# STU's products by disjoint segments of a block, with four stored sums of the mixed matrices

## The chip, the cores and the metric

The kernel runs on one core of a Trainium2 chip. The metric is the device time of one execution in microseconds, the median of several; everything is fp32. The engines named here are TensorE (matrix products, PE in the profile), VectorE (DVE), ScalarE (ACT), GpSimd (POOL) and SyncE (SP), which issues most of the transfers.

## The reference, cut to what matters

The input is a batch of 4 images of 48 x 48 tokens with 128 channels. A first layer (group norm, projection, depthwise convolution, four directional selective scans, gating) and an attention over the 2304 tokens come first. The change lies in the last part, an STU (a spectral filter bank) that runs on four prefixes of the sequence and adds the four results with weights:

```python
for i, frac in enumerate((1, 2, 4, 8)):
    xi = x[:, :T // frac]
    si = _stu(xi, sigma, phi, M_u[i], M_phi_plus[i], M_phi_minus[i])
    si = jnp.pad(si, ((0, 0), (0, T - si.shape[1]), (0, 0)))
    outs.append(si)
...
return jnp.sum(stacked * weights, axis=-1)
```

`_stu` convolves the tokens causally with 16 filters `phi`, in a plain and in an alternating form, multiplies each result by the 128 x 128 matrices `Mpp[k]` and `Mpm[k]` with weight `sigma**0.25`, and adds three products of delayed tokens with `Mu`. The convolution is causal, so its values don't depend on where a prefix ends; only the matrices differ. For a token at position t the result is therefore one product with the weighted sum of the matrices of those prefixes that hold t: all four in the first eighth (288 tokens), three up to a quarter (576), two up to a half (1152), one beyond.

## The kernel before, in words

Per batch the kernel runs a prologue, the scans, an epilogue with the attention, and the STU. The scans of batch b run beside other work for TensorE: beside those of batch 0 the matrices are mixed (`mixture`), beside those of batches 1, 2 and 3 runs the STU of the batch before. The STU of batch 3 runs alone at the end (`stu_alone`, the last stage).

The order on each engine is written out by hand. `scans` makes 192 steps per batch (24 chunks of 384 tokens with 8 units each). Each step has one scan unit: a product with `B` (VectorE at L450, or GpSimd for three units of eight), four decays on ScalarE (`dA`, L455), four scans on VectorE (L458), a product with `C` on GpSimd (L467) and a sum on TensorE (L475). At four points of a step the function `more` draws pieces of the accompanying work until that work has had its share of all TensorE columns. The total is 24 `CHUNK_COLS` (147456 columns) plus `MIX_COLS` or `STU_COLS`, so each step gets the same number of columns, whatever it takes in time.

The STU takes every fourth token as one column (576 columns in four residues). The columns are cut into five blocks, `BLOCKS`: 128, 128, 128, 128 and 64 wide. An item is one block with one filter `k`; there are 5 x 16 items per batch. An item has six convolution groups (`conv`, L978), each a chain of 128 x 256 matmuls (128 x 128 in the last block), one for every block up to this one. Their operand `tt` is fetched in a ring of four buffers (`fetch`, L948), and the matrices `G` of the item in a ring of two (`fetch_G`, L959), right behind the `tt` of three items later. After three groups of an item stands `project` of the item before (L1044): for each of two halves `q` the eight convolved pieces `U` are multiplied by `G`, and all 16 filters add into one bank of PSUM. `ar` (L1034) puts the products with `Mu` (tile `mue`) into the same bank at the start of a block. Copies of convolution results are made by ScalarE (L992, L1004), sums of them by VectorE (L1007).

Three of the places where a prefix ends fall inside a block: after 72 columns of block 0, 16 of block 1 and 32 of block 2 (`extra` in `BLOCKS`). The kernel before takes the product of the whole block with the sum of the matrices of all prefixes that hold the whole block, and adds for the first `extra` columns a product with the one matrix that holds only there. `parts(w, extra)` gives these two, (128, 1) and (extra, 0), the numbers 1 and 0 being matrices of the pair that was fetched. To serve them, DRAM keeps six matrices for each filter and half (`gd`) and for each delay (`mud`): three partial sums and three single ones.

`mixture` makes `gd`. For each filter and half it scales a unit matrix by the weights, on ScalarE (`W`, L821 and L822), and multiplies it with the matrices `M` (L835): twelve matmuls in two groups (j = 1 the sums, six matmuls of 384, 256 and 128 columns; j = 0 the single ones, six of 128 columns), two copies to `Gm` by ScalarE (L810) and one store (L812). The load of `M` (L817) is issued just ahead of the first matmul that uses it.

Of the kernel before, what the change touches and what calls it, by code (L numbers as in the profile page):

```python
# [8 lines left out]
F32 = mybir.dt.float32  # L9
AF = mybir.ActivationFunctionType  # L10
ALU = mybir.AluOpType
# [4 lines left out]
P = 128  # L16
B, H, W, C = 4, 48, 48, 128
# [8 lines left out]
KF = 16  # L26
NF = 4
# [6 lines left out]
SLOT = 2 * (LF + 1)  # L34


BLOCKS = [(0, 128, 0, 72), (128, 256, 2, 16), (256, 384, 4, 32), (384, 512, 5, 0), (512, 576, 5, 0)]
SHIFT = 55.0


# [14 lines left out]
def hybrid_kernel(ctx: ExitStack, tc: tile.TileContext, a: dict, out: bass.AP):  # L55
# [3 lines left out]
    nc = tc.nc  # L59
# [3 lines left out]
    res = ctx.enter_context(tc.tile_pool(name="res", bufs=1, space=DRAM))  # L63
# [70 lines left out]
    zs = res.tile([NH, P, L], F32, name="zd")  # L134
    td = res.tile([L, C], F32, name="td")
    ud = res.tile([P, 4, 1 + LF], F32, name="ud")
    gd = res.tile([KF, P, 2, 2 * NF - 2, C], F32, name="gd")
    mud = res.tile([P, 2 * NF - 2, 3, C], F32, name="mud")
    fd = res.tile([KF, 3, 2, LF + P], F32, name="fd")
    xdd = [[res.tile([P, CS], F32, name=f"xdd{k}_{c}") for c in range(L // CS)] for k in range(2)]  # L140

# [587 lines left out]

    MIX_COLS = KF * 2 * 2 * (6 + 3) * C

    ws = wp.tile([P, KF, NF], F32, name="ws")

    def weights(one):

        def load(name, shape, src):  # L740
            t = one.tile(shape, F32, name=name)
            nc.scalar.dma_start(t, src)
            return t

        lg = load("lg", [P, NF], a["log_weights"].partition_broadcast(P))
        gu = load("gu", [P, NF], a["gumbel"].partition_broadcast(P))
        sg = load("sg", [P, KF], a["sigma"].partition_broadcast(P))
        ph = load("ph", [KF, 2, 2, LF + P + 1], a["phi"])
        mu = load("mu", [P, NF, 3, C], a["M_u"].rearrange("i j d e -> d i j e"))
        for i in range(6):  # L750
            yield
        hard, wts = [one.tile([P, NF], F32, name=n) for n in ("hard", "wts")]
        m = one.tile([P, 2], F32, name="m")

        nc.vector.tensor_add(lg, lg, gu)
        nc.vector.tensor_reduce(m[:, 0:1], lg, AX.X, ALU.max)
        nc.vector.tensor_scalar(lg, lg, m[:, 0:1], None, ALU.subtract)
        nc.scalar.activation(lg, lg, AF.Exp)
        yield

        fc = one.tile([KF, 3, 2, LF + P], F32, name="fc")
        n = LF + P
        nc.vector.tensor_copy(fc[:, 0], ph[:, :, 0, :n])
        yield
        nc.vector.tensor_sub(fc[:, 1], ph[:, :, 1, 1:], ph[:, :, 0, :n])
        yield
        nc.vector.tensor_sub(fc[:, 2], ph[:, :, 1, :n], ph[:, :, 0, :n])
        nc.scalar.dma_start(fd, fc)
        yield
        nc.vector.tensor_reduce(m[:, 0:1], lg, AX.X, ALU.add)  # L770
        nc.vector.reciprocal(m[:, 0:1], m[:, 0:1])
        nc.vector.tensor_scalar_mul(lg, lg, m[:, 0:1])
        nc.vector.tensor_reduce(m[:, 0:1], lg, AX.X, ALU.max)
        nc.vector.tensor_scalar(hard, lg, m[:, 0:1], None, ALU.is_equal)
        nc.vector.memset(m[:, 1:2], 1.0)
        yield
        for i in range(NF):

            nc.vector.tensor_tensor(hard[:, i:i + 1], hard[:, i:i + 1], m[:, 1:2], ALU.mult)
            nc.vector.tensor_tensor(m[:, 1:2], m[:, 1:2], hard[:, i:i + 1], ALU.subtract)  # L780
        nc.vector.tensor_sub(wts, hard, lg)
        nc.vector.tensor_add(wts, wts, lg)
        yield

        quarter = one.tile([P, KF], F32, name="quarter")
        nc.vector.memset(quarter, 0.25)
        nc.gpsimd.tensor_tensor(sg, sg, quarter, ALU.pow)
        mum = one.tile([P, 2 * NF - 2, 3, C], F32, name="mum")
        nc.vector.tensor_scalar_mul(mum[:, 5], mu[:, 0], wts[:, 0:1])
        for i in range(1, NF):  # L790
            nc.vector.tensor_scalar_mul(mum[:, 6 - 2 * i], mu[:, i], wts[:, i:i + 1])
            if i < NF - 1:
                nc.vector.tensor_tensor(mum[:, 5 - 2 * i], mum[:, 7 - 2 * i], mum[:, 6 - 2 * i], ALU.add)
            yield
        nc.scalar.dma_start(mud, mum)
        for i in range(NF):
            nc.vector.tensor_scalar_mul(ws[:, :, i], sg, wts[:, i:i + 1])
        zero = one.tile([P, 4, 1], F32, name="zero")
        nc.vector.memset(zero, 0.0)
        nc.scalar.dma_start(ud[:, :, 0:1], zero)  # L800

    def mixture(pool, ps):

        late = []
        banks = [0]

        def keep_(G, p, j, k, q):
            nc.scalar.copy(G[:, :, j], p)  # L810
            if j == 0:
                nc.sync.dma_start(gd[k, :, q], G.rearrange("p s j c -> p (s j) c"))  # L812

        for k in range(KF):
            M = [pool.two.tile([P, NF, C], F32, tag=f"M{j}", name=f"M{j}_{k}") for j in range(2)]
            for t, src in zip(M, ("M_phi_plus", "M_phi_minus")):
                nc.sync.dma_start(t, a[src][:, k].rearrange("i d e -> d i e"))  # L817

            W = pool.two.tile([P, 2, NF, P], F32, tag="W", name=f"W{k}")
            for i in range(NF):  # L820
                nc.scalar.activation(W[:, 0, i], ident, AF.Copy, scale=ws[:, k, i:i + 1])  # L821
                nc.scalar.activation(W[:, 1, i], nident, AF.Copy, scale=ws[:, k, i:i + 1])  # L822
            yield 0
            for q in range(2):
                G = pool.two.tile([P, 3, 2, C], F32, tag="Gm", name=f"Gm{k}_{q}")
                for j in (1, 0):
                    p = ps.psc.tile([P, 3, C], F32, tag=("c", "q0", "q1")[banks[0] % 3], name=f"G{k}_{q}_{j}")
                    banks[0] += 1
                    for i in range(NF):

                        n = NF - 1 - i if j else 1
                        if i == (NF - 1 if j else 0):
                            continue
                        for t in range(2):
                            nc.tensor.matmul(p[:, :n] if j else p[:, NF - 1 - i], W[:, q if t else 0, i],  # L835
                                             M[t][:, i].unsqueeze(1).to_broadcast([P, n, C]) if j else M[t][:, i],
                                             start=(t == 0 and (i == 0 or not j)),
                                             stop=(t == 1 and (i == NF - 2 or not j)))
                            yield n * C
                    if late:  # L840
                        keep_(*late.pop())
                    late.append((G, p, j, k, q))
        keep_(*late.pop())

    def begin_stu(b):
# [6 lines left out]
    def tail(b, J, T, po, pool, ps):  # L852
# [38 lines left out]
        for j in range(4):  # L891
# [5 lines left out]
        nc.sync.dma_start(ud[:, :, 1 + P * J:1 + P * J + k], uT.rearrange("c (j p) -> c j p", j=4))  # L897

    STU_COLS = sum(KF * 12 * sum(hi - max(lo, J * P) for J in range((hi + P - 1) // P))
                   + (2 * KF + 3) * 4 * (hi - lo + extra) + 4 * (hi - lo) for lo, hi, place, extra in BLOCKS)  # L900

    def stu(b, pool, ps):

# [15 lines left out]
        tts, Gs, Q, U, now, nxt = {}, {}, {}, {}, {}, [0]  # L919
        late = []  # L920
        banks = {}
# [98 lines left out]

        def parts(w, extra):

            return ((w, 1), (extra, 0)) if extra else ((w, 0),)

        def ar(n):

            (lo, hi, place, extra), k = items[n]
            w = hi - lo
            p = ps.psp.tile([P, 512], F32, tag="p", name=f"pr{b}_{n}")
            now["p"] = p = p[:, :4 * w].rearrange("p (f r m) -> p f r m", f=2, r=2)  # L1030
            for i, (v, x) in enumerate(parts(w, extra)):
                for j in range(3):
                    src = now["x"][:, 2 - j:6 - j].rearrange("p (r f) m -> p f r m", f=2)
                    nc.tensor.matmul(p[:, :, :, :v], now["mu"][:, x, j, :], src[:, :, :, :v],  # L1034
                                     start=(i == 0 and j == 0), stop=False)
            yield 3 * 4 * (w + extra)

        def project(n):
            (lo, hi, place, extra), k = items[n]
            w = hi - lo  # L1040
            p = now["p"].rearrange("p f r m -> p (f r) m")
            for q in range(2):
                for v, x in reversed(parts(w, extra)):
                    nc.tensor.matmul(p[:, :, :v], Gs[n][:, q, x, :], U[n][:, 4 * q:4 * q + 4, :v], start=False,  # L1044
                                     stop=(k == KF - 1 and q == 1 and v == w))
                yield 4 * (w + extra)
            if k == KF - 1:
                late.append(lambda: kept(n, now["p"], w))

# [83 lines left out]
    for b in range(B):  # L1133
        sp = Stage(tc, f"h{b}", "left", s=(6, SB))
        ps = Stage(tc, f"b{b}", "right", psa=(2, PSUM), psy=(1, PSUM), psB=(1, PSUM), psc=(1, PSUM), psp=(1, PSUM))
# [106 lines left out]
```

## Time and profile before

The time is 6407.89 us, median of 3 runs from 6407.33 to 6413.88; the profiled execution spans 6402.6 us.

| | busy us | share of the span |
|---|---|---|
| TensorE | 5427.8 | 85% |
| VectorE | 4622.7 | 72% |
| GpSimd | 3840.5 | 60% |
| ScalarE | 2980.6 | 47% |

| group | instructions | busy us | mean ns |
|---|---|---|---|
| projections L1044, all forms | 2048 | 693.5 | 468 |
| products with `mue` L1034, all forms | 192 | 65.8 | 493 |
| mixing matmuls L835, 128 columns | 512 | 106.6 | 340 |
| mixing matmuls L835, 256 columns | 128 | 52.3 | 496 |
| mixing matmuls L835, 384 columns | 128 | 79.0 | 722 |
| `Gm` copies L810 | 64 | 30.0 | 470 |

An fp32 matmul of the program stands in the trace as two records, each with a weight load, so 2048 records are 1024 matmuls. A record's duration runs to the end of the matmul, which overlaps with the next one's start; what a matmul takes of TensorE is read from the distance between starts, or from the chain of waits. The profile cuts the span into 40 slices of 160 us and gives the busy share of each engine in tenths. Idle time is put down to what ended it.

### The profile page before, as it was taken

What the parts mean: (1) busy time and instruction counts of PE and PEld (TensorE: products, weight loads), DVE (VectorE), ACT (ScalarE), POOL (GpSimd) and SP (SyncE); (2) the same over time, 40 slices, a digit from 0 to 9 for tenths busy, and PEclk for the clock granted to TensorE, in tenths of its full rate; (3) what the DMA queues carried; (4) which work ended last, traced back from release to release, by engine and by line L of the source; (5) the groups of instructions that cost most, each with busy time, mean ns of one, the idle gap of its engine ahead of it and who ended that gap; (6) DMA issues with size and microseconds to landing.
All of it is one profiled execution on the core that took longest, in us unless ns stands there. A gap on an engine that the chain in (4) does not pass through costs nothing.

```text
span 6402.6 us, 75570 instructions
## 1 busy us (share of the span) xinstructions
PE 5427.8 (85%) x25032; PEld 3364.4 (53%) x25032; DVE 4622.7 (72%) x5553; ACT 2980.6 (47%) x5693; POOL 3840.5 (60%) x1825
## 2 busy tenths in 40 slices
PE   3665565697999998888999998788999998889999
PEld 1222222444556667544555666534555667547889
DVE  6999999548889998458899998458899998311000
ACT  2555555245555554245555554245555554232111
POOL 1988888406788887307788987207888987100000
PEclk6778777799999999899999999899999999899999
DMA  4556566127888888127888888127888887025546
GB/s 106 139 138 151 141 143 149 40 55 167 196 203 214 225 218 244 53 62 172 197 205 218 226 220 236 41 64 188 195 214 215 219 230 218 28 70 150 153 141 212
DMA packets 658246, 1033.52 MB, mean 161 GB/s; under 512 B 93856, under 2 KB 515872, under 8 KB 633120
## 3 DMA queue, kind: packets, MB, share of 16 engines
q1 hardware_dynamic: 652032, 1025.00, 62.3%
q10 hardware_dynamic: 5824, 3.69, 0.2%
q8 instruction: 200, 3.28, 0.2%
q14 instruction: 190, 1.56, 0.1%
HBM read 905.79 MB, written 122.56 MB: 161 GB/s over the span
## 4 chain that ended last, share of the span: by engine, by line
PE 49%; DVE 20%; DMA 17%; POOL 4%; issue 4%; ACT 4%; SPq 3%; DVEq 0%; ACTq 0%; POOLq 0%
PE cv L978 22%; DVE s L458 8%; PE pr L1044 7%; DMA tt<-fd 6%; DMA rep<-dtdud 4%; PE y L475 4%; DVE s L450 4%; PE s L714 4%; DMA bc<-xdd 3%; PE o L707 3%; POOL s L467 3%; PE B L442 2%; PE op L650 2%; DVE xc L264 2%; DMA G<-gd 2%
## 5 line engine op out<-in xcount | busy, mean ns | idle before, releaser
L467 POOL TENSOR_TENSOR s<-s,bc 128x1536 f32<-128x1536 f32 x768 | 2646.4, 3447 | 177.3 <-DVE s L458 93.3
L458 DVE TENSOR_TENSOR_SCAN s<-dA,carry,s 128x384 f32<-128x384 f32 x2560 | 2442.5, 1000 | 246.3 <-ACT dA L455 244.1
L455 ACT ACTIVATE dA<-rep,A 128x384 f32<-128x384 f32 x3072 | 1780.5, 585 | 1422.4 <-DVE s L458 1395.7
L978 PE MATMUL cv<-tt,u 128*128 128x256 f32 (+3 forms) x7680 | 1649.9, 354 | 131.2 <-DMA tt<-fd 68.1
L978 PEld LDWEIGHTS cv<-tt,u 128*128 128x128 f32 x7680 | 1271.9, 193 | 647.2 <-issue 309.2
L450 POOL TENSOR_TENSOR s<-rep,bc 128x1536 f32<-128x1536 f32 x288 | 993.9, 3451 | 93.0 <-DMA bc<-xdd 93.0
L450 DVE TENSOR_TENSOR s<-rep,B 128x1536 f32<-128x1536 f32 x480 | 832.7, 1735 | 78.3 <-PE B L442 47.1
L978 PE MATMUL cv<-tt,us 128*128 128x256 f32 (+3 forms) x3840 | 855.4, 352 | 35.2 <-DMA tt<-fd 26.0
L475 PE MATMUL y<-s,csum 128*32 128x384 f32 x6144 | 714.7, 540 | 139.7 <-DVE ya L481 75.8
L978 PEld LDWEIGHTS cv<-tt,us 128*128 128x128 f32 x3840 | 640.6, 192 | 228.9 <-issue 66.7
L1007 DVE TENSOR_TENSOR U<-cv,Q 128x256 f32<-128x256 f32 (+1 forms) x640 | 244.4, 382 | 688.3 <-PE cv L978 679.9
L1044 PE MATMUL pr<-U,G 128*128 128x512 f32 (+4 forms) x2048 | 693.5, 468 | 2.2 <-ACT U L1004 2.2
L442 PE MATMUL B<-xd,spread 128*128 128x384 f32 x960 | 446.9, 550 | 182.9 <-DVE s L450 173.1
L1004 ACT COPY U<-cv 128x256 f32<-128x256 f32 (+1 forms) x640 | 222.9, 348 | 676.1 <-PE cv L978 675.2
L458 DVE TENSOR_TENSOR_SCAN s<-dA,s 128x384 f32<-128x384 f32 x512 | 458.4, 941 | 77.1 <-ACT dA L455 76.1
L466 POOL COPY carry<-s 128x4 f32<-128x4 f32 x640 | 120.9, 189 | 560.8 <-DVE s L458 536.4
L1044 PEld LDWEIGHTS pr<-U,G 128*128 128x128 f32 x2048 | 336.3, 190 | 194.3 <-issue 140.4
L992 ACT COPY Q<-cv 128x256 f32<-128x256 f32 (+3 forms) x640 | 223.0, 348 | 378.7 <-PE cv L978 375.2
L714 PE MATMUL s<-xnT 128*128 128x512 f32 (+1 forms) x720 | 356.9, 581 | 44.7 <-ACT xnT L676 23.4
L158 POOL TENSOR_TENSOR ln_vu<-ln_vu,mhalf 128x4 f32<-128x4 f32 (+1 forms) x20 | 26.8, 1340 | 603.4 <-DVE ln_vu L157 603.4
L475 PEld LDWEIGHTS y<-s,csum 128*32 128x32 f32 x6144 | 126.7, 112 | 492.9 <-issue 328.7
L716 ACT ACTIVATE e<-s,shift 128x512 f32<-128x512 f32 (+1 forms) x360 | 230.9, 644 | 315.2 <-PE s L714 314.7
(158 smaller groups left out, 3976.5 us busy)
## 6 DMA issues: line engine op xcount, KB each, us to landing
rep<-dtdud SPq DMA_DIRECT2D x768, 384.0 KB, 7.7
tt<-fd SPq DMA_DIRECT2D x192, 577.0 KB, 5.3
bc<-xdd SPq DMA_DIRECT2D x2304, 48.0 KB, 3.4
tt<-fd SPq DMA_DIRECT2D x192, 513.0 KB, 4.7
tt<-fd SPq DMA_DIRECT2D x192, 385.0 KB, 4.3
dtdud<-re SPq DMA_DIRECT2D x768, 96.0 KB, 2.2
G<-gd SPq DMA_DIRECT2D x192, 256.0 KB, 5.6
tt<-fd SPq DMA_DIRECT2D x64, 514.0 KB, 5.9
```

The lines of the kernel that those rows point to most:

```text
L442: nc.tensor.matmul(self.bt[:, :CS], spread[:, self.ch.k // 2, self.q].rearrange("p c j -> p (c j)"), self.ch.xd, start=True, stop=True)
L450: eng.tensor_tensor(s, self.ch.rep[self.h][:, 1], bt.unsqueeze(1).to_broadcast([P, G4, CS]), ALU.mult)
L455: nc.scalar.activation(dA[:, :CS], ch.rep[self.h][:, 0, g], AF.Exp, scale=A[:, ch.k, self.h * G4 + g, self.q:self.q + 1])
L458: nc.vector.tensor_tensor_scan(s, dA[:, CS - 1::-1] if ch.rev else dA[:, :CS], s, 0.0 if ch.first else carry[:, self.h, self.q, g:g + 1], ...
L467: nc.gpsimd.tensor_tensor(self.s, self.s, ch.bc[Q4 + self.q].unsqueeze(1).to_broadcast([P, G4, CS]), ALU.mult)
L475: nc.tensor.matmul(ch.y[g * DL:(g + 1) * DL, :CS], csum, self.s[:, g], start=(self.q == 0), stop=(self.q == Q4 - 1))
L714: nc.tensor.matmul(p[:, :w], xnT[:, i * P:(i + 1) * P], xnT[:, 512 * J:512 * J + w], start=True, stop=True)
L716: nc.scalar.activation(e[:, :w], p[:, :w], AF.Exp, bias=shift)
L978: nc.tensor.matmul(p2[:, :, at - first:], x, t[:, :, hi - 1 - at + J * P:end if end >= 0 else None:-1], start=(c < 2 and J == 0), stop=(J ...
L992: nc.scalar.copy(Q[g], p[:, :2 * nw])
L1007: nc.vector.tensor_tensor(dst, src, q, ALU.add)
L1044: nc.tensor.matmul(p[:, :, :v], Gs[n][:, q, x, :], U[n][:, 4 * q:4 * q + 4, :v], start=False, stop=(k == KF - 1 and q == 1 and v == w))
```

## The change

Each block is cut where the prefix ends, into two segments that don't overlap, and each segment is multiplied once, by the sum of all the matrices that hold there. So `mixture` has to store four sums, one for each set of prefixes, in place of six matrices; they come out of one group of eight matmuls (512, 384, 256 and 128 columns, twice each), with one copy and one store. `parts` gives (first column, end, matrix). The flag that starts a group in PSUM is set on the first matmul of the first segment alone. The aim is to compute no column twice. The totals `MIX_COLS` and `STU_COLS`, from which the shares of the steps are worked out, follow. The sums of `mum` for the delays are made by one more addition.

```diff
-BLOCKS = [(0, 128, 0, 72), (128, 256, 2, 16), (256, 384, 4, 32), (384, 512, 5, 0), (512, 576, 5, 0)]
+BLOCKS = [(0, 128, 0, 72), (128, 256, 1, 16), (256, 384, 2, 32), (384, 512, 3, 0), (512, 576, 3, 0)]
...
-    gd = res.tile([KF, P, 2, 2 * NF - 2, C], F32, name="gd")
-    mud = res.tile([P, 2 * NF - 2, 3, C], F32, name="mud")
+    gd = res.tile([KF, P, 2, NF, C], F32, name="gd")
+    mud = res.tile([P, NF, 3, C], F32, name="mud")
...
-    MIX_COLS = KF * 2 * 2 * (6 + 3) * C
+    MIX_COLS = KF * 2 * NF * (NF + 1) * C
...
-        mum = one.tile([P, 2 * NF - 2, 3, C], F32, name="mum")
-        nc.vector.tensor_scalar_mul(mum[:, 5], mu[:, 0], wts[:, 0:1])
+        mum = one.tile([P, NF, 3, C], F32, name="mum")
+        nc.vector.tensor_scalar_mul(mum[:, NF - 1], mu[:, 0], wts[:, 0:1])
         for i in range(1, NF):
-            nc.vector.tensor_scalar_mul(mum[:, 6 - 2 * i], mu[:, i], wts[:, i:i + 1])
-            if i < NF - 1:
-                nc.vector.tensor_tensor(mum[:, 5 - 2 * i], mum[:, 7 - 2 * i], mum[:, 6 - 2 * i], ALU.add)
+            nc.vector.tensor_scalar_mul(mum[:, NF - 1 - i], mu[:, i], wts[:, i:i + 1])
+            nc.vector.tensor_tensor(mum[:, NF - 1 - i], mum[:, NF - 1 - i], mum[:, NF - i], ALU.add)
...
             for q in range(2):
-                G = pool.two.tile([P, 3, 2, C], F32, tag="Gm", name=f"Gm{k}_{q}")
-                for j in (1, 0):
-                    p = ps.psc.tile([P, 3, C], F32, tag=("c", "q0", "q1")[banks[0] % 3], name=f"G{k}_{q}_{j}")
...
-                    if late:
-                        keep_(*late.pop())
-                    late.append((G, p, j, k, q))
+                p = ps.psc.tile([P, NF, C], F32, tag=("c", "q0", "q1")[banks[0] % 3], name=f"G{k}_{q}")
+                banks[0] += 1
+                for i in range(NF):
+
+                    n = NF - i
+                    for t in range(2):
+                        nc.tensor.matmul(p[:, :n], W[:, q if t else 0, i],
+                                         M[t][:, i].unsqueeze(1).to_broadcast([P, n, C]),
+                                         start=(t == 0 and i == 0), stop=(t == 1 and i == NF - 1))
+                        yield n * C
+                if late:
+                    keep_(*late.pop())
+                late.append((p, k, q))
...
-                   + (2 * KF + 3) * 4 * (hi - lo + extra) + 4 * (hi - lo) for lo, hi, place, extra in BLOCKS)
+                   + (2 * KF + 3) * 4 * (hi - lo) + 4 * (hi - lo) for lo, hi, place, extra in BLOCKS)
...
-            return ((w, 1), (extra, 0)) if extra else ((w, 0),)
+            return ((0, extra, 0), (extra, w, 1)) if extra else ((0, w, 0),)
...
-                    nc.tensor.matmul(p[:, :, :, :v], now["mu"][:, x, j, :], src[:, :, :, :v],
-                                     start=(i == 0 and j == 0), stop=False)
-            yield 3 * 4 * (w + extra)
+                    nc.tensor.matmul(p[:, :, :, v0:v1], now["mu"][:, x, j, :], src[:, :, :, v0:v1],
+                                     start=(j == 0 and v0 == 0), stop=False)
+            yield 3 * 4 * w
...
-                for v, x in reversed(parts(w, extra)):
-                    nc.tensor.matmul(p[:, :, :v], Gs[n][:, q, x, :], U[n][:, 4 * q:4 * q + 4, :v], start=False,
-                                     stop=(k == KF - 1 and q == 1 and v == w))
-                yield 4 * (w + extra)
+                for v0, v1, x in parts(w, extra):
+                    nc.tensor.matmul(p[:, :, v0:v1], Gs[n][:, q, x, :], U[n][:, 4 * q:4 * q + 4, v0:v1], start=False,
+                                     stop=(k == KF - 1 and q == 1 and v1 == w))
+                yield 4 * w
```

More of the change, by code (lines that the diff above doesn't have):

```diff
@@ L807, in mixture, with keep_ @@
         banks = [0]
[L809 to L812, printed above, removed]
+        def keep_(p, k, q):
+            G = pool.two.tile([P, NF, C], F32, tag="Gm", name=f"Gm{k}_{q}")
+            nc.scalar.copy(G, p)
+            nc.sync.dma_start(gd[k, :, q], G)
         for k in range(KF):
@@ L824, in mixture @@
             for q in range(2):
-                G = pool.two.tile([P, 3, 2, C], F32, tag="Gm", name=f"Gm{k}_{q}")
-                for j in (1, 0):
-                    p = ps.psc.tile([P, 3, C], F32, tag=("c", "q0", "q1")[banks[0] % 3], name=f"G{k}_{q}_{j}")
[L828 to L839, printed above, removed]
-                    if late:
-                        keep_(*late.pop())
-                    late.append((G, p, j, k, q))
+                p = ps.psc.tile([P, NF, C], F32, tag=("c", "q0", "q1")[banks[0] % 3], name=f"G{k}_{q}")
[10 more added lines that the diff above has]
+                late.append((p, k, q))
         keep_(*late.pop())
@@ L1030, in ar @@
             now["p"] = p = p[:, :4 * w].rearrange("p (f r m) -> p f r m", f=2, r=2)
-            for i, (v, x) in enumerate(parts(w, extra)):
+            for v0, v1, x in parts(w, extra):
                 for j in range(3):
                     src = now["x"][:, 2 - j:6 - j].rearrange("p (r f) m -> p f r m", f=2)
-                    nc.tensor.matmul(p[:, :, :, :v], now["mu"][:, x, j, :], src[:, :, :, :v],
-                                     start=(i == 0 and j == 0), stop=False)
-            yield 3 * 4 * (w + extra)
+                    nc.tensor.matmul(p[:, :, :, v0:v1], now["mu"][:, x, j, :], src[:, :, :, v0:v1],
+                                     start=(j == 0 and v0 == 0), stop=False)
+            yield 3 * 4 * w
         def project(n):
@@ L1042, in project @@
             for q in range(2):
-                for v, x in reversed(parts(w, extra)):
-                    nc.tensor.matmul(p[:, :, :v], Gs[n][:, q, x, :], U[n][:, 4 * q:4 * q + 4, :v], start=False,
-                                     stop=(k == KF - 1 and q == 1 and v == w))
-                yield 4 * (w + extra)
+                for v0, v1, x in parts(w, extra):
+                    nc.tensor.matmul(p[:, :, v0:v1], Gs[n][:, q, x, :], U[n][:, 4 * q:4 * q + 4, v0:v1], start=False,
+                                     stop=(k == KF - 1 and q == 1 and v1 == w))
+                yield 4 * w
             if k == KF - 1:
```

## The prediction, on record before the changed kernel ran

> **What bounds the kernel now.** I read the busy slices first, then the chain of waits in the last stage, then the matmul groups there, and last the stretches and waits of a scan phase.
>
> ```profile
> PE   3665565697999998888999998788999998889999
> DVE  6999999548889998458899998458899998311000
> POOL 1988888406788887307788987207888987100000
> ```
>
> A slice is 160 us. Slices 1 to 7 are batch 0's scans, with the mixing of the matrices beside them. Slices 9 to 16, 18 to 25 and 27 to 34 are the scans of batches 1 to 3, with the STU of the batch before beside them: TensorE, VectorE and GpSimd are all at 8 or 9 tenths. From 35.5 on (5709 us) the STU of batch 3 runs alone and only TensorE is busy. The chain of waits there, in order of time (start, length, what):
>
> ```profile
> 5709.07 1.30 PE cv L978 x6
> 5710.37 2.69 PE pr L1044 x8
> 5713.06 2.61 PE cv L978 x12
> 5715.67 2.69 PE pr L1044 x8
> 5718.36 2.61 PE cv L978 x12
> ```
>
> The chain of the lone stage's first block holds TensorE and nothing else: six convolution matmuls (2.61 us) and four projections (2.69), 5.30 us per filter, sixteen times. Each fp32 matmul leaves two records, so x8 is four matmuls. So 2 x (512 + 288) columns take 2.69 us: 1.68 ns per column. In the second block the chain gives 2.16 us for 2 x (512 + 64) columns, in the third 2.16 for 2 x (512 + 128), in the fourth 1.72 for 2 x 512. Thus 512 columns cost 0.86 us, and the 64 column piece costs 0.22, as much as the 128 column one: a floor.
>
> Now the scan phase of batch 1. The stretches are blocks 0 to 4 of the STU, cut where the first products with `mue` of each block stand (busy us by engine, clock, DMA share, GB/s):
>
> ```profile
> 1480.00:1630.00 150.00, 135.03 (x580) 73.47 (x579) 129.97 (x156) 89.06 (x180) 117.73 (x59) 1.00 0.78 181
> 1630.00:1842.00 212.00, 200.33 (x920) 118.56 (x919) 188.72 (x216) 120.27 (x236) 172.72 (x77) 0.98 0.81 198
> 1842.00:2105.00 263.00, 249.20 (x1183) 153.51 (x1182) 242.28 (x270) 150.18 (x280) 220.63 (x100) 0.97 0.85 214
> 2105.00:2395.00 290.00, 279.31 (x1372) 177.54 (x1370) 274.55 (x305) 170.25 (x312) 258.19 (x120) 0.99 0.86 220
> 2395.00:2560.00 165.00, 144.80 (x1037) 114.56 (x1038) 133.29 (x153) 74.77 (x161) 122.97 (x60) 0.93 0.88 244
> ```
>
> TensorE looks 90 to 96% busy, but a lone matmul's record holds its drain (0.38 us for 256 columns, against 0.217 between starts in the lone stage). By columns it is less. A phase has 192 scan steps, and `more` gives each an equal share of columns: (147456 + 406944) / 192 = 2887, which at 1.68 ns is 4.86 us. A step takes 150/25.0 = 6.0 us in block 0, then 6.4, 5.8, 5.3 and 5.9. VectorE (third pair) is really busy 87, 89, 92, 95 and 81%. Its idle time comes through ScalarE. The waits of 1480 to 2560 us (who waited for whom, us, times, longest):
>
> ```profile
> ACT U L1004 <- PE cv L978: 103.1, 81, 8.1
> DVE s L458 <- ACT dA L455: 86.6, 74, 7.7
> ...
> PE cv L978 <- DMA tt<-fd: 23.7, 14, 5.1
> ```
>
> ScalarE stands behind a copy that TensorE has not fed, the next decay `dA` is queued behind it, and the scan waits for that.
>
> [...]
>
> **The change, part by part.**
>
> *Projections (L1044).* The number of matmuls stays. Block 0: 512 + 288 columns become 288 + 224, so 288 fewer per pair; block 1: 512 + 64 become 64 + 448; block 2: 512 + 128 become 128 + 384. Together 480 columns per pair, 32 pairs per batch: 15360 x 1.68 ns = 25.8 us. The 64 column piece sat on its floor before and stays there, so nothing is lost. The autoregressive products (L1034): 3 x 480 columns, 2.4 us. Sum 28.2 us of TensorE per batch.
>
> *Lone stage.* TensorE alone is on the path, so all of it counts unless something else takes over. In block 0 that is `G`. It is issued 0.6 us after an item's first convolution (5730.70 against 5730.1) and its weight load stands 1.1 us after the next item's first one. An item may then not be shorter than the landing less 0.4 us. The fifteen landings of block 0 range from 3.7 to 6.1 us, mean 5.0, since 387 KB of `tt` are issued 0.4 us ahead of each. Today's 5.30 us allow 5.7; the new item of 2.61 + 1.72 = 4.33 would allow only 4.7. With the transfers of an item (643 KB) packed closer, I take 5.2 for the landing, so 4.8 us per item: 16 x 0.5 = 8 us instead of 15.5. Bounds: all 15.5, or 3 if the landing becomes 5.5. Block 1 gives 16 x 2 x 64 x 1.68 ns = 3.4, block 2 6.9, L1034 2.4. Lone stage: -20.7 (-16 to -28).
>
> *Three scan phases.* STU columns per batch fall to 390144, hence 2800 columns per step, 0.147 us less. But the 192 steps are shared out anew. Of a step's columns 2887 - 768 = 2119 were STU's, now 2032. By columns, the blocks had 25.0, 32.9, 45.6, 55.1 and 33.3 steps, and get 21.2, 33.3, 45.4, 57.4 and 34.8. Block 0: more items fall on a step (0.75 for 0.64), each with about 1.6 us of VectorE adds (four of 0.40) and 643 KB, so 6.2 us a step: 21.2 x 6.2 = 131 against 150, -18.6. Blocks 1 and 2: two thirds of the 0.147 is felt: 33.3 x 6.34 and 45.4 x 5.67, -0.9 and -5.6. Block 3: VectorE is 95% busy and its work per step does not fall; 5.22 us for 5.26, and 2.3 steps more: +9.6. Block 4: `tt` at 244 GB/s is the limit; its bytes stay, and 1.5 steps more of about 0.6 MB scan data cost +3.5. Sum -12 per phase, -36 for three. Bounds: 0 if VectorE holds every block, -28 each if TensorE does.
>
> *Mixture (L835).* Twelve matmuls with 2304 columns become eight with 2560: 8192 columns more, 14 us of TensorE, where it has room (30 busy us in 50). Two copies of 0.47 us become one of 512, 0.585 (ScalarE's copies of 512 at L1052): 11 us off ScalarE. The first matmul still waits for `M` just issued ahead of it (57.8 us in 12 waits); behind it on TensorE stand `B` and `y`, and VectorE waits for `B`. The wait does not move, the burst after it grows by a tenth: +2 (-10 to +15).
>
> *Nothing:* one more VectorE add for `mum` and smaller stores of `gd` and `mud`, hidden in the prologue and beside the scans. Reads of `G` and `mue` keep count and run length.
>
> Sum: -20.7 - 36 + 2 = -55, so 6353.
>
> **The rivals.**
> *A. TensorE is the bound everywhere.* For it: the slices show it at 9, and projections lie on the chain of the scan phases with 7.7%. Against: 4.86 us of columns in a step of 5.3 to 6.4. Time: 4 x -28.2 + 2 = -111, 6297.
> *B. VectorE holds the scan phases.* For it: 95% in block 3, no VectorE work removed. Against: 86.6 us waiting for ScalarE. Only the lone stage gains: -20.7 + 2 = -19, 6389; with `G` later still, 6394.
> *C. Slower than before.* The denser first block crowds the transfers: those of `rep` and `bc` are 8.7% of the scan phases' chain (94 us each); a tenth longer is +9 per phase, 28 in all; each of 16 waits for `M` 1 us longer, +16; lone stage -13. Sum +31, 6439. For it: DMA share 0.78 to 0.88. Against: its bytes do not grow.
>
> **How the numbers follow.** Forecast 0.61, A 0.12, B 0.20, C 0.07. The forecast spreads about 25 us round 6353. The range 6315 to 6391 holds it and most of B, and leaves out A and C. The lone stage's gain stands in all cases but C, so faster by over 0.2% (13 us) 0.90, within 0.04, slower 0.06.
>
> **What would show it.** In the lone stage: items of block 0 at 4.8 us with short TensorE waits for `G`, of block 1 at 7.1, of block 2 at 9.5, and 1.72, 1.95 and 1.72 us for the four projections. In the scan phases: block 0 near 131 us, block 3 near 300, VectorE's busy sum unchanged near 1000 us per phase. Mixture: eight matmuls per half filter, waits for `M` still near 60 us. I am wrong if segments inside a bank cost more than 1.68 ns a column, if `G` stretches block 0 to its old 5.3 us, or if the shifted shares of columns change VectorE's idle time by more than 10 us per phase.

## The result, and the profile after

The changed kernel takes 6360.56 us (median of 4 runs, 6358.27 to 6368.86), the kernel before 6407.61 (median of 4, 6394.97 to 6413.88). The ratio is 0.9935, 95% interval 0.9921 to 0.9949: 0.65% faster, 47 us. The forecast was 6353, its range 6315 to 6391.

The slices look much as before:

```profile
PE   3666566697999998897999998787999998789999
DVE  6999999657899997558999997458899998311000
POOL 1898988405888987306888987306788987200000
```

No slice of the three engines moves by more than a tenth, so they can't tell where the time went. Where the 45.3 us between the two profiled spans (6402.6 and 6357.3) lie can be read from GpSimd's products with `C` (L467), which frame each scan phase: 192 of them, one per step. The answers of the traces for batch 3, kernel before and kernel after (first and last start at the end of each line):

```profile
L467 POOL TENSOR_TENSOR s<-s,bc x192: 3422/3449/3477, 4332.9 to 5447.3; 128x1536 f32<-128x1536 f32 x192
```

```profile
L467 POOL TENSOR_TENSOR s<-s,bc x192: 3417/3452/3488, 4319.5 to 5427.8; 128x1536 f32<-128x1536 f32 x192
```

The phase took 1114.4 us and takes 1108.3. All stretches, read the same way:

| stretch | before | after | difference |
|---|---|---|---|
| scans of batch 0, with the mixture | 1034.2 | 1035.3 | +1.1 |
| scans of batch 1 | 1119.1 | 1109.1 | -10.0 |
| scans of batch 2 | 1116.3 | 1110.8 | -5.5 |
| scans of batch 3 | 1114.4 | 1108.3 | -6.1 |
| the stretches between them, together | | | +1.0 |
| from the last scan to the end | 955.3 | 929.5 | -25.8 |

So over half of the gain is the lone stage's, a quarter of the work removed. Its first block in the chain of waits of the kernel after:

```profile
5725.59 1.97 PE pr L1038 x8
5727.55 2.61 PE cv L972 x12
5730.16 1.73 PE pr L1038 x8
5731.89 2.61 PE cv L972 x12
```

Against the chain of before, the convolutions stand at 2.61 us and the four projections have gone from 2.69 to 1.73: 512 columns per pair at 1.68 ns, with no price for the cut. Seven of the sixteen items, in places every second one, have 1.89 to 1.97: they are held up by `G`, their first weight load of the projections starting 0.1 us after `G` has landed. Only one item is held up for long:

```profile
5701.42 6.26 DMA G<-gd
5707.68 0.14 issue
5707.81 1.97 PE pr L1038 x8
```

The 6.26 us are the whole transfer, from issue to landing; TensorE itself stood still for 1.2 us of it.

Between the first products with `mue` of one block and the next, the lone blocks 1 and 2 went from 124.0 to 120.2 and from 165.4 to 158.0 us, and block 3 stayed at 192.9.

The scan phase of batch 1 after the change, cut as before where the first `mue` products of a block stand:

```profile
1479.00:1610.00 131.00, 117.95 (x561) 75.70 (x559) 113.75 (x141) 78.83 (x168) 103.37 (x51) 0.97 0.84 192
1611.00:1823.00 212.00, 196.68 (x895) 117.09 (x895) 187.79 (x216) 120.94 (x233) 169.81 (x76) 0.95 0.81 199
1824.00:2080.00 256.00, 239.01 (x1183) 151.17 (x1181) 239.73 (x267) 149.47 (x279) 220.00 (x100) 0.99 0.86 216
2081.00:2376.00 295.00, 281.44 (x1387) 177.05 (x1385) 284.05 (x315) 174.05 (x319) 269.47 (x124) 1.00 0.85 218
2377.00:2550.00 173.00, 146.60 (x1046) 114.41 (x1045) 138.92 (x158) 78.09 (x165) 126.80 (x62) 0.92 0.85 239
```

Block 0 is a sixth shorter, blocks 3 and 4 are longer, though nothing was added to them. By columns they got more of the 192 steps. VectorE (third pair) is busy 96% in block 3, before 95%. The waits of that phase, 1479 to 2550 us:

```profile
ACT U L998 <- PE cv L972: 85.6, 73, 5.2
DVE s L458 <- ACT dA L455: 67.7, 67, 3.4
```

ScalarE waits 85.6 us for convolutions in place of 103.1, and VectorE 67.7 us for ScalarE in place of 86.6. In the phases of batches 2 and 3 VectorE's wait went from 82.5 to 61.3 and from 82.7 to 67.0 us. So VectorE's waiting has shrunk by the path that the prediction named. In block 4 another wait has grown. The waits there in the phase of batch 1, before (2397 to 2595 us) and after (2377 to 2585 us):

```profile
PE cv L978 <- DMA tt<-fd: 16.7, 8, 5.1
DVE s L450 <- PE B L442: 1.2, 2, 1.0
```

```profile
PE cv L972 <- DMA tt<-fd: 20.8, 8, 5.0
DVE s L450 <- PE B L442: 7.6, 3, 4.8
```

TensorE waits longer for `tt`, and VectorE waits for the product `B` that TensorE makes.

### The profile page after: what moved, and what is told of

It is laid out like the page before. It is cut to its first block, busy times and chain, and to the rows that moved or that the text cites. A ratio compares the mean times of both kernels' runs of the same rounds, so it can differ in the third digit from the quotient of the medians.

```text
span 6357.3 us, 75050 instructions
## 1 busy us (share of the span) xinstructions
PE 5346.4 (84%) x24776; PEld 3336.7 (52%) x24776; DVE 4622.3 (73%) x5554; ACT 2973.4 (47%) x5661; POOL 3843.0 (60%) x1825
## 4 chain that ended last, share of the span: by engine, by line
PE 43%; DVE 21%; DMA 21%; ACT 4%; issue 4%; SPq 4%; POOL 3%; DVEq 0%; ACTq 0%; POOLq 0%
PE cv L972 19%; DVE s L458 10%; DMA tt<-fd 7%; DMA rep<-dtdud 6%; PE pr L1038 5%; DVE s L450 4%; DMA bc<-xdd 4%; PE s L714 4%; PE y L475 3%; PE o L707 3%; DMA G<-gd 2%; PE op L650 2%; POOL s L467 2%; PE B L442 2%; DVE xc L264 2%
## 5 line engine op out<-in xcount | busy, mean ns | idle before, releaser
L467 POOL TENSOR_TENSOR s<-s,bc 128x1536 f32<-128x1536 f32 x768 | 2647.2, 3449 | 165.6 <-DVE s L458 78.3
L450 POOL TENSOR_TENSOR s<-rep,bc 128x1536 f32<-128x1536 f32 x288 | 994.7, 3454 | 93.2 <-DMA bc<-xdd 93.2
L450 DVE TENSOR_TENSOR s<-rep,B 128x1536 f32<-128x1536 f32 x480 | 832.8, 1735 | 91.3 <-PE B L442 61.6
L1038 PE MATMUL pr<-U,G 128*128 128x288 f32 (+7 forms) x2048 | 596.4, 422 | 7.5 <-DMA G<-gd 5.9
```

Of the source, the lines that this page charges most:

```text
L450: eng.tensor_tensor(s, self.ch.rep[self.h][:, 1], bt.unsqueeze(1).to_broadcast([P, G4, CS]), ALU.mult)
L467: nc.gpsimd.tensor_tensor(self.s, self.s, ch.bc[Q4 + self.q].unsqueeze(1).to_broadcast([P, G4, CS]), ALU.mult)
L1038: nc.tensor.matmul(p[:, :, v0:v1], Gs[n][:, q, x, :], U[n][:, 4 * q:4 * q + 4, v0:v1], start=False, stop=(k == KF - 1 and q == 1 and v1 == w))
```

## The experiments

All times are of the profiled runs unless a median or ratio is named; the blocks are means over the three scan phases, and each ratio is to the kernel before on the same chip. "More share" and "block 4 two steps" have the early `G` too, and the latter the old shares. Of each edit the lines that matter are shown.

| kernel | block 0 | 1 | 2 | 3 | 4 | phase | ratio, 95% interval |
|---|---|---|---|---|---|---|---|
| before | 156.3 | 205.0 | 263.0 | 291.0 | 199.0 | 1116.6 | 1 |
| after | 131.6 | 211.5 | 259.1 | 297.4 | 207.9 | 1109.4 | 0.9935 [0.9921, 0.9949] |
| mixture alone | 156.3 | 206.0 | 261.9 | 290.8 | 200.5 | 1118.5 | 1.0010 [1.0003, 1.0016] |
| old shares | 146.5 | 204.2 | 258.1 | 293.0 | 199.9 | 1104.2 | 0.9915 [0.9901, 0.9928] |
| early `G` | 128.6 | 211.9 | 260.7 | 298.0 | 214.6 | 1116.2 | 0.9955 [0.9942, 0.9967] |
| early `G`, old shares | 146.3 | 203.3 | 257.2 | 289.4 | 197.9 | 1096.6 | 0.9887 [0.9872, 0.9902] |
| half the products | 125.1 | 195.2 | 266.4 | 297.8 | 213.8 | 1100.8 | 0.9804 [0.9790, 0.9817] |
| the same, shares kept | 129.5 | 206.4 | 254.3 | 294.0 | 210.1 | 1096.7 | 0.9778 [0.9762, 0.9795] |
| draws shifted | 133.4 | 212.9 | 257.1 | 296.5 | 207.5 | 1109.4 | 0.9936 [0.9923, 0.9949] |
| more share | 165.9 | 204.2 | 261.3 | 282.9 | 208.6 | 1123.7 | 0.9995 [0.9987, 1.0003] |
| block 4 old steps | 133.9 | 209.9 | 258.1 | 304.9 | 200.3 | 1109.6 | 0.9929 [0.9916, 0.9941] |
| block 4 two steps | 153.0 | 210.0 | 259.0 | 292.3 | 207.2 | 1123.9 | 1.0001 [0.9993, 1.0009] |

**One part alone: the mixture.** STU's products are those of before, with the new `mixture`.

```diff
-            return ((0, extra, 0), (extra, w, 1)) if extra else ((0, w, 0),)
+            return ((w, 1), (extra, 0)) if extra else ((w, 0),)
```

> The mixture of four sums as in the changed kernel, but STU's products as before (whole block, then the first columns again), with the old totals; the products then use sums where single matrices belong, so the output is not the reference's. Theory (the gain is the STU's): the mixture phase within 3 us of before, everything behind it as before, total within 0.1% of 6408. Rival (the shorter mixture brings part of the gain): 10 us or more below before, all of it before 1170 us.

The mixture phase was 1038.8 us (+4.6), the total 0.1% above before. The four stored sums alone save no time; they are what the segments need. The gain is the STU's.

**Less work in the same steps.** The pieces report the old columns, and `STU_COLS` follows.

```diff
-                yield 4 * w
+                yield 4 * (w + extra)
```

> The changed kernel, but its pieces report the columns of before (width plus extra), so each block of the STU gets as many scan steps as before (25.0, 32.9, 45.6, 55.1, 33.3) and only the work on TensorE inside the steps is less. Theory (blocks 3 and 4 are held by VectorE and by transfers, and grow because they get more steps): blocks 3 and 4 back to about 291 and 198 us, block 0 at about 145 us, phase 1105 us or so, the same as or up to 6 us per phase below the changed kernel; total 6345 to 6362. Rival (block 0 gains only because it gets fewer steps): block 0 near 154 us, phase near 1115 us, total near 6380. Rival A (TensorE is the bound): phase about 1090 us, total 6300 to 6320.

The theory held: blocks 3 and 4 are back at 293 and 200 us, block 0 is at 146.5, the phase 5 us below the changed kernel, the median 6348.69. That VectorE and transfers hold blocks 3 and 4 this run doesn't show. The rival that would have block 0 gain only by its fewer steps fell (146.5, not 154), and so did TensorE as the bound (1104, not 1090).

**What a phase feels of TensorE.** The products of the second half `q` are left out, 62 us of TensorE per batch, first with the shares following, then with the shares kept.

```diff
-            for q in range(2):
+            for q in range(1):
```

> The changed kernel without the products of the second half q of the filters (36864 columns per batch left out, 62 us of TensorE; output not the reference's); shares follow. It measures how much of TensorE's columns a scan phase feels. Theory (a quarter to a third, since VectorE and transfers hold the rest): 15 to 22 us less per scan phase than the changed kernel; the lone stage 50 to 62 us less, with waits for G in block 0; total 6360 - 110 = 6250. Rival A (TensorE holds the scan phases): 62 us per phase, total about 6115. Rival B (VectorE alone holds them): under 5 us per phase, total about 6300.

```diff
-                for v0, v1, x in parts(w, extra):
+                for v0, v1, x in parts(w, extra) if q == 0 else ():
```

> The changed kernel without the products of the second half q (62 us of TensorE per batch; output not the reference's), but reporting their columns, so that every block keeps the scan steps it has in the changed kernel. With the shares moved the scan phases felt only 14% of it. Theory (the move of steps into blocks 3 and 4 ate part of it): with the shares kept 15 to 30 us less per scan phase than in the changed kernel, more in block 0 than elsewhere; total 6240 to 6265. If it is again 9 us or less, the scan phases feel TensorE's columns little, wherever the steps lie.

With the shares following, the phases fell by 8.6 us on average, below what was expected: blocks 2 and 4 grew. With the shares kept they fell by 12.7 us (12.8, 10.6, 14.8), 20% of the 62, just under the range expected. The lone stage fell by some 56 us of 62 in both. So a scan phase feels about a fifth of the columns taken from all its blocks; the lone stage nearly all. The fifth isn't a constant: of the 28.2 us that the change takes from TensorE per batch (the prediction's sum) a phase felt 12.4, or 44%, with the old shares, 9.8 of it in block 0, which lost most columns.

**What a phase feels of VectorE.** One VectorE instruction more per step, that nothing waits for; in a second run with two inputs.

```diff
+            nc.vector.tensor_scalar_mul(spare, spare, 1.0)
```

> The changed kernel with one idle VectorE instruction more in each of the 192 steps of each scan phase (192 elements wide, on a tile of its own, nothing waits for it). It measures how much of VectorE's time a scan phase feels. Its duration is read from the trace, probably 0.2 to 0.3 us, 40 to 55 us per phase. Theory (VectorE is the nearest bound in blocks 0 to 3): 60 to 90% of it shows in each of the three phases, total 6360 + 4 x 35 = 6500 with the mixture phase. Rival A (TensorE holds them): under 30% of it, total about 6400.

```diff
+            nc.vector.tensor_tensor(spare[:, 0], spare[:, 0], spare[:, 1], ALU.mult)
```

> As the run with the VectorE load, but the added instruction has two inputs (192 elements wide, on a tile of its own) and should not be held up for microseconds as that one was. Its duration is read from the trace, probably 0.25 to 0.4 us, so 50 to 75 us per phase. Theory (VectorE is the nearest bound of the scan phases): half to nine tenths of what it adds to VectorE shows in the time, total 6360 + 4 x 40 = 6520. If TensorE or the transfers hold the phases: under a third, total below 6430.

Both totals were far off (7044.92 and 7117.33), because the instruction takes not 0.3 but 1.3 and 1.4 us on average; the form with two inputs, expected not to be held up, is held up as well. The groups of the first and of the second:

```profile
L569 DVE TENSOR_SCALAR spare<-spare 128x192 f32<-128x192 f32 x776 | 1029.3, 1326 | 0.1
```

```profile
L569 DVE TENSOR_TENSOR spare<-spare 128x192 f32<-128x192 f32 x776 | 1113.2, 1435 | 0.1
```

As a share the expectation held: of the 1029.3 us added to VectorE, 685.7 show in the span (67%), of the 1113.2, 757.1 (68%). But most of the added time is a wait for GpSimd (last section), and the load is four times what was planned. With it VectorE is busy 97% of a scan phase, this wait included, for 90% in the changed kernel: of its idle time, some 110 us per phase, about 35 are left, and what the load didn't take from there had to show. So VectorE's bound is close; what a phase feels of a little VectorE time isn't shown, and the 67% can't be set against the fifth above.

**The order alone.** Two draws of each step a twentieth of a step earlier.

```diff
-            more((s + 0.25) / len(units))
+            more((s + 0.2) / len(units))
...
-            more((s + 0.75) / len(units))
+            more((s + 0.7) / len(units))
```

> The changed kernel with two of the four draws of a step a twentieth of a step earlier; the work and the blocks' shares stay. It shows how far a scan phase moves by the order of instructions alone. Theory: within 5 us per phase of the changed kernel, total 6345 to 6375. If the phases move by 10 us or more, the gains of 5 to 10 us per phase in the other runs can't be put down to a cause.

The phases were 1109.4, 1108.9 and 1109.8 us, at most 2 us from the changed kernel's. Differences of 5 us per phase are more than this one shuffle makes.

**`G` earlier.** The next item's `G` is fetched behind the fourth convolution.

```diff
-                if i == 0:
-                    fetch_G(n)
+                if i == 0 and n == 0:
+                    fetch_G(0)
+                elif i == 3:
+                    fetch_G(n + 1)
```

> The changed kernel with G of the next item fetched half an item earlier (behind the fourth convolution of the item before, as soon as its buffer is free). Theory (in the lone block 0 the landing of G lengthens some items, 0.2 us each and 2.2 us once): all lone items of block 0 at 4.33 us, block 0 at about 70.5 instead of 75.2 us; scan phases within 5 us of the changed kernel, total 6345 to 6362. Rival (the longer items come from something else, for instance the clock or the segments' width): the lone block 0 stays at 75 us.

> Both: G fetched half an item earlier, and the old shares of the steps. Theory: the two add up, 5 to 20 us below the changed kernel, total 6340 to 6355. If the old shares alone bring nothing, the total is that of the early G alone.

In the lone block 0 the waits are gone. The chain of the run with early `G`:

```profile
5724.05 1.73 PE pr L1038 x8
5725.77 2.61 PE cv L972 x12
5728.38 1.73 PE pr L1038 x8
5730.11 2.61 PE cv L972 x12
5732.72 1.73 PE pr L1038 x8
```

All items take 4.34 us, and the block 72.4 us for 75.2 (the 70.5 expected left out the block's ends). So `G` was what lengthened some items. But the scan phases grew by 7 us, mostly in block 4, and the total was above the changed kernel's. With the old shares the same edit gave the fastest kernel that still does all the products, median 6323.98, ratio 0.9887: phases at 1096.6, below both parts alone. The parts don't add up, and the total lies below the 6340 to 6355 expected.

**Where the steps go.** Still more steps for the cut blocks; then only block 4's steps changed.

```diff
-                yield 4 * w
+                yield 4 * (w + 2 * extra)
```

> Early G, and still more steps for the blocks with a cut: pieces report width plus twice extra (27.7, 32.5, 45.9, 53.5 and 32.5 steps). Theory (items of block 0 are dearer than their columns tell, since each brings four additions on VectorE): another 2 to 5 us less per phase than with the old shares and early G, total near 6312 to 6322. If the old shares were already the best, 0 to 10 us more.

```diff
+    SHARE = {512: 0.9487}
...
-            yield 2 * (hi - at)
+            yield 2 * (hi - at) * SHARE.get(lo, 1)
```

> The changed kernel, but the pieces of block 4 report 0.9487 of their columns, so that this block alone goes back to its old 33.3 of the 192 steps (34.8 in the changed kernel), and the other four share 1.5 steps more. Theory (a block's time is its number of steps times its time per step): block 4 at about 199 instead of 208 us, the others about 8 us longer together, phases within 4 us of the changed kernel, total 6350 to 6370. Rival (block 4 is slow at some spacings of its items and quick at others, and the number of steps does not tell): block 4 anywhere between 198 and 215, or the others unchanged, and the phases 5 us or more away from the changed kernel.

```diff
+    SHARE = {512: 0.9698}
...
+                yield 4 * (w + extra) * SHARE.get(lo, 1)
```

> Early G and the old shares, but the pieces of block 4 report 0.9698 of their columns, so that an item of block 4 gets 2.03 steps in place of 2.08, as in the run with still more steps for the cut blocks, where block 4 took 206 to 211 us. Theory (steps times time per step): block 4 at about 193, the others 4 us longer, total within 8 us of 6324. Rival (items close to two steps apart are slow): block 4 at 205 us or more, total 6345 or more.

The first missed widely: 27 us slower per phase than with early `G` and the old shares, and the whole gain was gone. The steps named in its expectation were worked out wrong: by the columns that the edit reports they are 28.6, 32.7, 45.8, 52.9 and 32.0. Block 0 rose by 20 us for 3.6 steps more, which is no more than its time per step; but block 4 rose by 11 although it had 1.3 steps fewer.

The second came out as the theory said: with 33.3 steps block 4 is at 200.3, the others are 7 us longer together, the phase is unchanged. The third came out as its rival said: with 2.03 steps per item block 4 takes 207 us, where 2.08 give 198; the total is 6402.2. Blocks 0 and 1 rose by 7 us each there too, with hardly any change of their steps. So a block's time isn't only its steps times a fixed time per step: some spacings of items against steps are slow, and the second run, which set block 4 back to the 2.08 steps per item of before, fits that as well as the theory.

The traces of all twelve kernels in the table show what goes with a slow block 4. In the five kernels with 2.08 steps per item it takes 196.8 to 202.4 us, and VectorE waits there for TensorE, for `B` or for a convolution, 6.6 to 13.1 us per phase. In the other seven it takes 205.2 to 216.5 us, and VectorE waits 14.7 to 33.6 us. TensorE's own wait for `tt` is mostly longer there too, 20.8 to 38.1 us for 12.8 to 22.5. This places the lost time, but no run changed `tt` alone, so the cause of the longer waits isn't shown. Nor is it settled what slows blocks 0 and 1.

## Why the prediction was right, point by point

**Projections.** Right: 480 columns fewer per pair at 1.68 ns. The four projections of an item take 1.73, 1.95 and 1.74 us in blocks 0 to 2, forecast 1.72, 1.95, 1.72. The 64 column piece still takes 0.22 us: the 1.95 us of block 1, less 2 x 448 columns at 1.68 ns (1.51 us), leave 0.44 for two such pieces.

**The second segment.** The forecast kept the number of matmuls: the second segment, which has no flag, got none of its own ahead of it. None was added: TensorE has 24776 records for 25032, and the 256 that are gone are the mixture's (512 for 768). What the flag does inside the bank stands in no trace; that part of the forecast was the author's assumption.

**Lone stage.** Mechanism right, size off: -20.7 forecast, -25.8 measured from the last scan. `G` does lengthen block 0, but less than assumed: the block fell by 12.5 us (87.8 to 75.2), not 8, because the landings stayed at 5.0 us, where 5.2 was taken, and only seven of the sixteen items were late. The run with early `G` puts its cost at 2.8 us. Blocks 1 and 2 gave 3.7 and 7.4 as forecast, with their part of L1034. Another 3.1 us lie in the first `mue` products, 5.96 us before and 2.83 after. By columns (3 x 288 x 1.68 ns) half of that, 1.5, is the change's; the rest goes with the granted clock in those microseconds, 0.72 before and 1.00 after (with early `G` it was 0.62 and they took 4.51). No run shows that the change brought the higher clock, so these 1.6 us count as luck.

**Scan phases.** Direction and the path of the waits right, size off by 5 us per phase: -12 forecast, -7.2 measured. Over three phases that is 14 us less than forecast, and the lone stage's 5 us more gave back only a part. The term that failed is block 4. It was put at +3.5, "the limit" being `tt`'s bytes at 244 GB/s; it is +8.9. The rate did not hold: it fell to 239 GB/s, while VectorE waited more for TensorE there. The block's time per step stayed at 6.0 us (199.0 for 33.3 steps, 207.9 for 34.8), but the run with 2.03 steps per item shows that the count of steps alone doesn't set it. The other blocks came out within 3 us of the forecast ends: 131.6 for 131, 211.5 for 211, 259.1 for 257, 297.4 for 300. In blocks 0 and 1 that is in part luck. Their starting points had been cut some 6 us wrong (150 and 212 for 156 and 205), which cancels in the sum. So the step of block 0 didn't grow from 6.0 to 6.2 us with denser items: it was 6.25 before and is 6.21. And block 1, forecast to gain 0.1 us per step, lost 0.1 (6.23 to 6.35). Of the three signs of being wrong none came: the columns cost 1.68 ns, `G` left block 0 most of its gain, and the shifted shares cost 5.2 us per phase (1109.4 for 1104.2), not 10, with VectorE's busy time unchanged.

**Mixture.** +2 forecast, +1.1 measured (+4.6 with the mixture alone). The waits for `M` grew from 57.8 to 73.7 us and weren't felt one for one.

**The rivals.** A fell: 20 to 44% of the columns taken from TensorE are felt in the scan phases, not all. B was too strong: VectorE's bound is close, and its busy time per phase stayed at 1004 us, but the phases did fall, and by 12.4 us with the old shares. C fell for the change itself; yet two runs, both with early `G`, show that other shares of steps can bring the kernel back to its old time.

## What to carry to other kernels

Removing work from TensorE gave here 20 to 44% of that work in the scan phases, where TensorE looked 88 to 96% busy before but other engines and the queues are in the chain of waits too, and some 56 of 62 us in the lone stage, where it stands alone in the chain; price the two separately. When work is spread over steps by a count of columns, changing the count moves other work too. Here two fifths of what the scan phases could have gained (7.2 against 12.4 us per phase) went that way: block 0, with 3.8 steps fewer than with the old shares, was 14.9 us shorter, and the other four blocks, with as many more, were 20.6 longer together. Try the removal with the old shares first.

## What the runs showed of the hardware that was not expected

A small VectorE instruction between SBUF tiles was held up by GpSimd. In the timeline of the run with two inputs:

```profile
1000.83 3.43 POOL L469 TENSOR_TENSOR s<-s,bc 128x1536 f32<-128x1536 f32 x1
1002.23 2.24 DVE L569 TENSOR_TENSOR spare<-spare 128x192 f32<-128x192 f32 x1
```

GpSimd's product ends at 1004.26, VectorE's 192 elements, begun at 1002.23, at 1004.47. The same instruction takes 0.32 us at least, with a median of 1.60 and at most 3.60; the form with one input 0.22, 1.49 and 3.50. It is the same throughout the trace: 742 of the 776 begin more than 0.02 us after a GpSimd product has begun and before it ends, and every one of them ends after it, by 0.21 to 0.35 us. With one input it is 746 of 776, by 0.11 to 0.19 us. Those that begin outside such a product, or within its first 0.02 us, take 0.32 to 0.35 and 0.22 to 0.27 us.

The kernel's own products on VectorE (L450), which read `B` from PSUM, show nothing of the kind: in the changed kernel all 480 take 1.72 to 1.77 us, and many begin and end within one GpSimd product. One of 1.73 us, for example, begins at 169.00, while GpSimd's runs from 167.82 to 171.27. Why these are not held up and the added instruction is, the runs don't show.
